# One region in place of five tanh buffers, in the additive attention of a two-layer block

## Chip, cores and metric

The kernel runs on one core of a Trainium2 chip. The metric is the device time of one execution in microseconds (us); less is better. Engines are named as in the profile: PE is TensorE (PEld its weight loads), DVE is VectorE, ACT is ScalarE, POOL is GpSimd, SP is SyncE, which issues most of the DMAs. All data is float32.

## The reference

`x` has shape (8, 64, 16, 128): 8 batches of N = 1024 tokens with 128 channels. Two layers follow each other, batch by batch except for the last step.

```python
# layer 0: attention with 8 heads over (m, g), two softmaxes, then a feed-forward part
scores = einsum('bhlfc,bhmgc->bhlfmg', q, k) / sqrt(c)
a = softmax(softmax(scores, axis=4), axis=5)
z = einsum('bhlfmg,bhmgc->bhlfc', a, v)          # then @ wo.T, + x, layer norm
x = layer_norm(relu(z1 @ w1.T + b1) @ w2.T + b2 + z1)

# layer 1: additive attention, for all pairs of tokens i, j
Wi = einsum('bnd,ed->bne', B, W)                 # B = layer norm of the tokens t
scores = einsum('d,bijd->bij', v, tanh(Wi[:, None] + Wi[:, :, None]))
t = t + softmax(scores, axis=-1) @ B

# then a recurrence over the tokens, y = sigmoid(wx_t + y @ V.T), with batch statistics
```

The costly part of layer 1 is the tanh of every pair of tokens. Since tanh(Wi_i + Wi_j) is the same for (i, j) and (j, i), the kernel computes only about half of the square.

## The kernel before

**Who orders the work.** Nothing is issued in a loop's order. `layer0`, `check_bounds`, `layer1` and `fetch_wx` only describe operations: `add` in `class Plan` takes for each the engines that may do it with a cost in us on each, a function that issues its instructions, what it reads and writes, and a priority. `Plan.emit` then plays the whole program through once, as the kernel is built. It keeps a modelled time for every engine, always takes the engine that can begin earliest and, of the operations that could begin on it within 0.15 us, the one with the least priority number, and issues it. What comes out is one fixed order of instructions for each engine; on the chip each engine works it off in order and waits where data or buffers aren't ready. Layer 0 of batch b+1 is thus woven into layer 1 of batch b.

**Buffers in the plan.** An operation with `take=` needs a buffer, one with `give=` frees it. A `Bank` names the buffers that it may choose from. `start_at` puts off an operation until the first of them is free in the plan, and `emit` takes the one that has been free longest:

```python
t = max(t, min(bank_free.get(c[0], 0.0) for c in take.of(e)))
...
take.name, take.tile = min(take.of(e), key=lambda c: bank_free.get(c[0], 0.0))
bank_free[take.name] = never
```

When the operation with `give=` is planned, the buffer counts as free from that operation's planned end, plus 0.6 us where PE does it. On the chip the real accesses to the columns decide: who writes columns waits for the matmuls that read them last.

**The pairs of tokens.** Tokens are in blocks of 128, `it` = 0 to 7. For block `it` only columns from its start on are needed, w = 1024 - 128 it of them. Four rows of a block (c = 0 to 3) are worked on at once, and k = max(1, 1024 // w) steps of r0 together; that is a *group*, `group` (L1006): 4k rows, whose first columns are left out as r0 grows (`begin`), so that a group has k(4w - 16 r0 - 6) columns for r0 over 0, and 4kw for r0 = 0. There are 172 groups in a batch, 1376 in all. A group goes through four steps:

1. It takes a tanh buffer `th` of 4N = 4096 columns (`slot`).
2. It is filled. Either POOL or DVE adds to `wiT` one column of it for each row (`add_rows`, L1039, for all k rows of one c; `add_row`, L1033, one row on DVE), or ACT does each row, sum and tanh in one instruction (`tanh_row`, L1029, the column as a bias). If ACT does row 0 it does all four; otherwise POOL and DVE share them.
3. If POOL or DVE filled it, ACT takes the tanh of the whole group in one instruction (`wide_tanh`, L1087).
4. PE multiplies each row by v (`times_v`, L1107), with results in the PSUM tile `sa`, and gives the buffer back.

**Stages.** In batches 1 to 6 the blocks are worked on in stages (0), (1, 7), (2, 6), (3, 5), (4), two blocks of a pair being interleaved. A stage ends with the Exp of its scores (`exps`, L1203, ACT). In batches 0 and 7 the stages are (4), (5, 7), (6), (0), (1), (2), (3), and the first three of batch 0 may use only three of the five buffers, since the other two hold the values of layer 0's eight heads then (`ths[3 + h // 4]` in `layer0`). The five buffers also hold four weights at the start (`early`) and x of all batches for `check_bounds`.

**Layer 0 beside it.** For each head and 128 tokens: scores on PE (L869), Exp on ACT (L872), sums and division on DVE (L876, L877, L880), a second Exp on ACT (L890), sums and reciprocal on DVE (L893, L894), a division on POOL (L904), transposes on PE (L783) with copies on DVE (L795), and the product with the values on PE (L918).

Of the kernel before, what the change touches and what calls it, by code (L numbers as in the profile page):

```python
# [15 lines left out]
P = 128  # L16
# [382 lines left out]
class Bank:  # L399
# [3 lines left out]
    def __init__(self, *choice, own=None):  # L403
        self.choice = choice
        self.own = own or {}
# [4 lines left out]
    def __call__(self):  # L410
        return self.tile


class Plan:

# [44 lines left out]
    def emit(self, slack=0.15, switch=0.1, stay=0.015):  # L460
        ops, by = self.ops, self.by
        after = [[] for _ in ops]
        left = []
        for n, o in enumerate(ops):
            before = o[4] | set(o[7])
            left.append(len(before))
            for d in before:
                after[d].append(n)
        engines = list(self.LATENCY)
        open_ = {e: [] for e in engines}  # L470
        free = dict.fromkeys(engines, 0.0)
        done = [0.0] * len(ops)
        began = [0.0] * len(ops)
        places = [None] * len(ops)
        mode = "full"
        bank_free = {}
        port_free = 0.0
        never = float("inf")
        self.order = []

        def ready_at(n, e):
            t = max((began[d] for d in ops[n][7]), default=0.0)
            for d in ops[n][4]:
                t = max(t, done[d] + (self.AGAIN if by[d] == e else self.LATENCY).get(by[d], 0.0))
            return t

        def start_at(n, t, e):
            take = ops[n][5]
            if take:
                t = max(t, min(bank_free.get(c[0], 0.0) for c in take.of(e)))  # L490
            if e == "POOL" or (e == "DVE" and ops[n][8]):
                t = max(t, port_free)
            return max(t, free[e])

        def release(n):
            where = ops[n][0]
            where = where() if callable(where) else where
            if where is None:
                began[n] = done[n] = ready_at(n, None)
                finish(n)  # L500
                return
            places[n] = {p[0]: (*p[1:], 0.0) for p in (where if isinstance(where, list) else [where])}
            for e in places[n]:
                open_[e].append((n, ready_at(n, e)))

        def finish(n):
            for a in after[n]:
                left[a] -= 1
                if left[a] == 0:
                    release(a)  # L510

        for n in [n for n, c in enumerate(left) if c == 0]:
            release(n)
        while any(open_.values()):
            first, e = min(
                (min(start_at(n, t, e) for n, t in open_[e]), i) for i, e in enumerate(engines) if open_[e]
            )
            assert first < never
            e = engines[e]
            n, start = min(  # L520
                ((n, s) for n, s in ((n, start_at(n, t, e)) for n, t in open_[e]) if s <= first + slack),
                key=lambda c: (ops[c[0]][2][0] + places[c[0]][e][1] + (stay if e == "PE" and ops[c[0]][3] != mode else 0), c[0]),
            )
            _, fn, _, m, _, take, give, _, port = ops[n]
            if take:
                take.name, take.tile = min(take.of(e), key=lambda c: bank_free.get(c[0], 0.0))
                bank_free[take.name] = never
            cost = places[n][e][0]
            if e == "PE":
                if m != mode:  # L530
                    cost += switch
                mode = m
            free[e] = start + (cost if e != "SP" else 0.2)
            if e == "POOL" or (e == "DVE" and port):
                port_free = start + cost
            began[n], done[n], by[n] = start, start + cost, e
            for q in places[n]:
                open_[q] = [c for c in open_[q] if c[0] != n]
            if give:
                bank_free[give.name] = done[n] + self.LATENCY[e]  # L540
            self.order.append((n, e, start, done[n]))
            fn(e)
            finish(n)
# [22 lines left out]
def fast_path(ctx: ExitStack, tc: tile.TileContext, a: dict, fits):  # L566
# [6 lines left out]
    NB, N, C = a["x"].shape  # L573
# [15 lines left out]
    work = main.enter_context(tc.tile_pool(name="work", bufs=1))  # L589
    psum = main.enter_context(tc.tile_pool(name="psum", bufs=1, space=PSUM))  # L590

    def tile_of(pool, name, shape):
        return pool.tile(shape, F32, tag=name, name=name)

    def ring(name, n, shape, pool=work):
        return [tile_of(pool, f"{name}{i}", shape) for i in range(n)]
# [17 lines left out]
        return t  # L614

    xTs = ring("xT", 2, [P, N])
    ths = ring("th", 5, [P, 4 * N])
    us = [wx[:, i, :] for i in range(2)]
    vps = [wx[:, 2 + i, :].rearrange("p (t c) -> p t c", c=C) for i in range(2)]
    aTs = ring("aT", 2, [P, NT, 2 * P])  # L620
# [16 lines left out]


    def early(k, name, eng):
        t = ths[k // 4][:, (k % 4) * N : (k % 4 + 1) * N].rearrange("p (h c) -> p h c", c=C)  # L640
        eng.dma_start(out=t, in_=a[name])
        return t

# [158 lines left out]
    def layer0(b):  # L802
# [16 lines left out]
        for n_part, part in enumerate(parts):  # L819
# [3 lines left out]
            for h in range(H):  # L823
                L0 = pace(n_part, h)

                u, vp, kvp = us[h % 2], vps[h % 2], ("vp", h % 2)
                if alone:
                    vp, kvp = ths[3 + h // 4][:, h % 4 * N : (h % 4 + 1) * N].rearrange("p (t c) -> p t c", c=C), ("vp0", h)
                for s in range(2) if part is None else (part,):
                    cols = slice(s * 512, (s + 1) * 512)  # L830

# [22 lines left out]
                for qt in qts:  # L854
                    L0 = pace(n_part, h + (qt - qts[0]) / len(qts))
                    i = (n_part * H + h) * len(qts) + qt - qts[0]
# [3 lines left out]
                    e, ke = e2[:, q, :], ("e", pair, q)  # L860
# [38 lines left out]
                    for q in range(2):  # L899
                        e, ke = e2[:, q, :], ("e", pair, q)  # L900
# [35 lines left out]
            for qh in range(2) if part is None else (part,):  # L936
# [4 lines left out]
                def raw(bank=bank):  # L941
# [4 lines left out]
                    take=bank, wait=[kg])  # L946
# [54 lines left out]
                add(("POOL", 2.2), affine2, r=[kg], w=[kg], pri=L0)  # L1001

    unused = stats[5][:, 3, 8:9]
    slots = [(f"th{s}", ths[s]) for s in range(5)]

    def group(it, at0, r0, k, wiT, all_wi, L1, ROWS, fillers, chain, left, both, first_half):  # L1006

# [5 lines left out]
        w = N - i0  # L1013
        g = count.setdefault("group", 0)
        count["group"] = g + 1
        slot = Bank(*slots[: 3 if first_half else 5])

        begin = [0 if r0 == 0 else 4 * r0 + c for c in range(4)]
        at = [k * sum(w - q for q in begin[:c]) for c in range(5)]

        def rows(c):
            return slot()[:, at[c] : at[c + 1]].rearrange("p (r n) -> p r n", r=k)
# [5 lines left out]
        def tanh_row(c, r):  # L1028
            nc.scalar.activation(rows(c)[:, r, :], wiT[:, i0 + begin[c] :], AF.Tanh, bias=w_i(c, r))  # L1029

        def add_row(c, r):

            nc.vector.tensor_scalar(  # L1033
                rows(c)[:, r, :], wiT[:, i0 + begin[c] :], w_i(c, r), 0.0, ALU.add, ALU.add, accum_out=unused
            )

        def add_rows(eng, c):
            shape = [P, k, w - begin[c]]
            eng.tensor_tensor(  # L1039
                rows(c), wiT[:, i0 + begin[c] :].unsqueeze(1).to_broadcast(shape),  # L1040
                w_i(c).unsqueeze(2).to_broadcast(shape), ALU.add,
            )
# [3 lines left out]
        work = {  # L1046
            "ACT": lambda c: (k * (0.18 + 0.833e-3 * (w - begin[c])), lambda: [tanh_row(c, r) for r in rows_of]),
            "POOL": lambda c: (0.27 + 1.62e-3 * k * (w - begin[c]), lambda: add_rows(nc.gpsimd, c)),
            "DVE": lambda c: (k * (0.21 + 1.05e-3 * (w - begin[c])), lambda: [add_row(c, r) for r in rows_of])
            if k < 4  # L1050
            else (0.15 + 1.04e-3 * k * (w - begin[c]), lambda: add_rows(nc.vector, c)),
        }
# [43 lines left out]
        for s0 in range(0, N, 512):  # L1096
            for c in range(4):
                s, s1 = max(s0, at0 + begin[c]), min(s0 + 512, at0 + w)
# [16 lines left out]
        n = -(-w // 512)  # L1115
# [18 lines left out]
    E_first, at = {}, 0  # L1134
# [153 lines left out]
    def check_bounds():  # L1288
# [1 line left out]

        cols, n2 = ET[:, 1, : 4 + 2 * H], ET[:, 2, : NB * NT]
        for b in range(NB):
            xb = ths[b // 4][:, b % 4 * N : (b % 4 + 1) * N].rearrange("p (t c) -> p t c", c=C)
            add(
                ("SP", 8.0),
                lambda _, b=b, xb=xb: nc.sync.dma_start(out=xb, in_=a["x"][b].rearrange("(t p) c -> p t c", p=P)),
                w=[("xn", b)], pri=LATE,
            )
            for t in range(NT):

                def square(_, xt=xb[:, t, :], j=b * NT + t):
                    nc.scalar.activation(xt, xt, AF.Square, accum_out=n2[:, j : j + 1])

                add(("ACT", 0.4), square, r=[("xn", b)], w=[("n2", b, t)], pri=LATE)
# [36 lines left out]
        for i, dst in enumerate((most, tot)):  # L1341
            through_bank(
                lambda bank, i=i: nc.tensor.matmul(
                    bank[0:1, :K], red[:, i : i + 1], ident[:K, :K], start=True, stop=True
                ), 0.3, ["red"],
# [17 lines left out]

    layer0(0)
    check_bounds()
    for b in range(NB):
        if b + 1 < NB:
# [38 lines left out]
    with tc.tile_pool(name="ps_w", bufs=2, space=PSUM) as ps_w, tc.tile_pool(  # L1406
# [22 lines left out]
        n = 0  # L1429
        for b in range(NB):  # L1430
            for g in range(2):
                pt = ps_t.tile([P, 4, C], F32, tag="yt", name="yt")
                for i in range(4):
                    t = 4 * g + i
# [75 lines left out]
```

## Time and profile before

| | us |
|---|---|
| median of 3 runs | 5395.53 (5393.81 to 5401.85) |
| the profiled execution | 5395.36, of which its span is 5393.6 |
| ACT busy | 5099.2 |
| PE busy | 5044.0 |
| DVE busy | 4933.6 |
| POOL busy | 4496.0 |
| wide tanh L1087, 953 instructions | 2629.0 |
| rows on ACT L1029, 2084 instructions | 1502.5 |
| rows on POOL L1039, 2268 instructions | 3318.7 |
| rows on DVE L1033, 1754 instructions | 1542.3 |

The profile is of one execution. The span runs from its first to its last instruction. The page gives the busy time of each engine, the same in 40 equal slices (135 us each), the chain of work that ended last, and the costliest groups of instructions with the idle time of the engine just before them and what ended it. The list of waits gives who waited for whom, in total, how often, and the longest. PE's ends are modelled, and busy PE isn't PE at its peak.

### The profile page before, as it was taken

To read this page: it belongs to the slowest core of one execution; us is meant where nothing else is said; L and a number is where in the kernel's file an instruction comes from. 1 tells how busy PE (TensorE), PEld (TensorE's weight loads), DVE (VectorE), ACT (ScalarE), POOL (GpSimd) and SP (SyncE) were. 2 spreads that over 40 slices of the span, in tenths; PEclk is the share of its full clock that TensorE was granted. 3 is DMA by queue.
4 is the path that set the end of the run, shared out by engine and by line. 5 is a ranking of instruction groups with operands and counts; after the bars stand their busy time and mean duration, and the time that the engine had idled before them with its cause. 6 is when DMAs were issued, how large, how long until landed. Compare 5 with 4: busy or idle time off the path is not lost.

```text
span 5393.6 us, 99434 instructions
## 1 busy us (share of the span) xinstructions
PE 5044.0 (94%) x39173; PEld 2771.6 (51%) x39173; DVE 4933.6 (91%) x8326; ACT 5099.2 (95%) x4190; POOL 4496.0 (83%) x3078
## 2 busy tenths in 40 slices
PE   8999999999999999999999999999999999995566
PEld 6655554555555455555555555545555455542125
DVE  7998989899999999899998999999998999999886
ACT  5489999999999999999999999999999999999994
POOL 2364779798989899899998989898898998996992
PEclk9999999999999999999999999999999999998999
DMA  2000000000000000000000000000000000000001
GB/s 62 1 5 1 1 1 5 1 9 1 1 5 6 4 1 1 5 9 1 1 5 5 5 1 1 5 5 5 1 1 3 7 1 1 1 30 8 1 1 68
DMA packets 27341, 37.73 MB, mean 7 GB/s; under 512 B 2512, under 2 KB 19280, under 8 KB 26864
## 3 DMA queue, kind: packets, MB, share of 16 engines
q1 hardware_dynamic: 24832, 27.99, 1.6%
q8 instruction: 310, 5.08, 0.4%
q10 hardware_dynamic: 1872, 3.16, 0.2%
q14 instruction: 167, 1.37, 0.1%
q0 software_dynamic: 160, 0.13, 0.0%
HBM read 19.22 MB, written 12.06 MB: 6 GB/s over the span
## 4 chain that ended last, share of the span: by engine, by line
PE 56%; ACT 19%; DVE 18%; issue 6%; POOL 1%; DMA 0%; DVEq 0%; ACTq 0%; SPq 0%; POOLq 0%
PE sa L1107 20%; PE m L918 11%; PE sc L869 10%; ACT th L1087 10%; PE m L783 6%; ACT th L1029 5%; DVE th L1033 5%; DVE stat_e L876 2%; DVE stat_e L893 2%; DVE wx L880 2%; ACT sc L872 2%; ACT wx L890 2%; PE m L1236 2%; DVE aT L795 2%; PE m L847 1%
## 5 line engine op out<-in xcount | busy, mean ns | idle before, releaser
L1039 POOL TENSOR_TENSOR th<-wiT 128x1024 f32<-128x1024 f32 (+54 forms) x2268 | 3318.7, 1500 | 318.2 <-PE sa L1107 298.8
L1087 ACT ACTIVATE th<-th 128x4096 f32<-128x4096 f32 (+55 forms) x953 | 2629.0, 2788 | 22.6 <-DVE th L1039 9.5
L1107 PE MATMUL sa<-th,vpat 128*32 128x512 f32 (+33 forms) x24576 | 2037.4, 462 | 235.6 <-ACT th L1087 223.3
L1033 DVE TENSOR_SCALAR_CACHE_REDUCE th<-wiT 128x512 f32<-128x512 f32 (+57 forms) x1754 | 1542.3, 879 | 156.7 <-PE sa L1107 40.3
L1029 ACT ACTIVATE th<-wiT 128x384 f32<-128x384 f32 (+60 forms) x2084 | 1502.5, 792 | 29.2 <-PE sa L1107 28.9
L1107 PEld LDWEIGHTS sa<-th,vpat 128*32 128x32 f32 x24576 | 662.8, 110 | 1372.1 <-issue 844.3
L904 POOL TENSOR_TENSOR wx<-wx,stat_e 128x1024 f32<-128x1024 f32 x512 | 983.9, 1944 | 389.4 <-DVE stat_e L894 320.8
L869 PE MATMUL sc<-xT,wx 128*128 128x512 f32 x2048 | 981.2, 604 | 11.3 <-DVE wx L880 10.7
L918 PE MATMUL m<-aT,wx 128*128 128x256 f32 x3584 | 823.7, 383 | 4.7 <-DVE aT L795 4.5
L918 PEld LDWEIGHTS m<-aT,wx 128*128 128x128 f32 x3584 | 668.1, 190 | 187.5 <-issue 48.0
L880 DVE TENSOR_TENSOR wx<-sc,stat_e 128x1024 f32<-128x1024 f32 x512 | 624.2, 1219 | 25.0
L876 DVE TENSOR_REDUCE stat_e<-sc 128x16 f32<-128x1024 f32 x512 | 619.7, 1210 | 25.8 <-ACT sc L872 25.3
L795 DVE COPY aT<-m 128x512 f32<-128x512 f32 x927 | 600.3, 674 | 36.7 <-PE m L783 34.3
L783 PEld LDWEIGHTS m<-ident,wx 128*128 128x128 f32 x3940 | 443.5, 141 | 326.0 <-issue 156.9
L893 DVE TENSOR_REDUCE stat_e<-wx 128x128 f32<-128x2048 f32 x256 | 583.2, 2278 | 19.1 <-ACT wx L890 18.4
L783 PE MATMUL m<-ident,wx 128*128 128x128 f32 x3940 | 562.6, 278 | 29.7 <-DVE aT L795 14.3
L872 ACT ACTIVATE sc<-sc 128x1024 f32<-128x1024 f32 x512 | 512.7, 1007 | 62.3 <-PE sc L869 56.0
L869 PEld LDWEIGHTS sc<-xT,wx 128*128 128x128 f32 x2048 | 354.7, 190 | 374.4 <-issue 329.3
L890 ACT ACTIVATE wx<-wx 128x2048 f32<-128x2048 f32 x256 | 487.7, 1905 | 30.1 <-DVE wx L880 29.9
L894 DVE RECIPROCAL stat_e<-stat_e 128x128 f32<-128x128 f32 x256 | 243.9, 953 | 8.8
L847 PEld LDWEIGHTS m<-Wvo,xT 128*128 128x128 f32 x1080 | 134.4, 192 | 53.0 <-issue 26.9
L847 PE MATMUL m<-Wvo,xT 128*128 128x128 f32 x1080 | 145.5, 281 | 4.4 <-DVE aT L795 2.4
(183 smaller groups left out, 2887.0 us busy)
## 6 DMA issues: line engine op xcount, KB each, us to landing
xT<-in_xt_dram SPq DMA_DIRECT2D x8, 512.0 KB, 3.6
th<-in_x_dram SPq DMA_DIRECT2D x8, 512.0 KB, 6.8
parked<-X SPq DMA_DIRECT2D x16, 256.0 KB, 2.3
xr<-parked SPq DMA_DIRECT2D x8, 512.0 KB, 8.1
parked_wx<-bT SPq DMA_DIRECT2D x14, 256.0 KB, 2.0
wx<-parked_wx SPq DMA_DIRECT2D x7, 512.0 KB, 4.3
out_dram<-ot ACTq DMA_DIRECT2D x8, 256.0 KB, 2.1
out_dram<-ot SPq DMA_DIRECT2D x8, 256.0 KB, 2.8
```

The costliest lines, as they stand in the source:

```text
L783: nc.tensor.transpose(bank[:, i * P : (i + 1) * P], s, ident)
L795: nc.vector.tensor_copy(dst, src)
L869: nc.tensor.matmul(sc[:, cols], u[:, qt * P : (qt + 1) * P], xT[:, cols], start=True, stop=True)
L876: nc.vector.tensor_reduce(r1, sc.rearrange("p (m g) -> p g m", g=G), AX.X, ALU.add)
L880: nc.vector.tensor_tensor(e3, sc3, r1.unsqueeze(1).to_broadcast([P, M, G]), ALU.mult)
L904: nc.gpsimd.tensor_tensor(e3, e3, r2[:, q, :].unsqueeze(2).to_broadcast([P, M, G]), ALU.mult)
L918: nc.tensor.matmul(bank()[:, :256], vp[:, t, :], aT[:, t, :], start=t == 0, stop=t == NT - 1)
L1029: nc.scalar.activation(rows(c)[:, r, :], wiT[:, i0 + begin[c] :], AF.Tanh, bias=w_i(c, r))
L1033: nc.vector.tensor_scalar(rows(c)[:, r, :], wiT[:, i0 + begin[c] :], w_i(c, r), 0.0, ALU.add, ALU.add, accum_out=unused)
L1039: eng.tensor_tensor(rows(c), wiT[:, i0 + begin[c] :].unsqueeze(1).to_broadcast(shape), w_i(c).unsqueeze(2).to_broadcast(shape), ALU.add,)
L1087: nc.scalar.activation(slot()[:, a:z], slot()[:, a:z], AF.Tanh)
L1107: nc.tensor.matmul(sa[32 * c : 32 * c + 32, s:s1], vpat[:, 31 - r0 - r : 63 - r0 - r], rows(c)[:, r, s - at0 - begin[c] : s1 - at0 - begin ...
```

## The change

The five tiles `ths` become one tile `th` of the same 20N columns. A `Room` keeps a list of spans of it, each with the time from which it is free in the plan. A group takes a `Span` with just as many columns as it has: `place` looks, from every border between spans, for neighbouring spans that together are long enough, and returns the place with the earliest start and, among equals, the lowest column. `hold` cuts the spans to fit, `free` sets the time from which the taken one is free again. `Bank` gets methods of the same names, so that `emit` asks either kind; what it does for PSUM banks stays the same. The limit of three buffers in the first stages becomes a limit of 12N columns.

```diff
+class Room:
+    def __init__(self, tile, size):
+        self.tile = tile
+        self.spans = [[0, size, 0.0]]
+
+    def place(self, n, now, top):
+        best = None
+        for i, (a, _, _) in enumerate(self.spans):
+            t, z = now, a
+            for _, z, free in self.spans[i:]:
+                t = max(t, free)
+                if z - a >= n:
+                    break
+            if z - a >= n and a + n <= top and (best is None or (t, a) < best):
+                best = (t, a)
+        return best
+
+    def hold(self, a, n):
+        spans = []
+        for x, z, t in self.spans:
+            if x < a:
+                spans.append([x, min(z, a), t])
+            if z > a + n:
+                spans.append([max(x, a + n), z, t])
+        spans.append([a, a + n, float("inf")])
+        self.spans = sorted(spans)
+
+    def free(self, a, t):
+        for span in self.spans:
+            if span[0] == a:
+                span[2] = t
+
+class Span:
...
+    def __call__(self):
+        return self.room.tile[:, self.at : self.at + self.n]
+
+    def when(self, e, t, bank_free):
+        return self.room.place(self.n, t, self.top)[0]
+
+    def hold(self, e, t, bank_free):
+        self.at = self.room.place(self.n, t, self.top)[1]
+        self.room.hold(self.at, self.n)
...
@@ Plan.emit
-                t = max(t, min(bank_free.get(c[0], 0.0) for c in take.of(e)))
+                t = take.when(e, t, bank_free)
...
-                take.name, take.tile = min(take.of(e), key=lambda c: bank_free.get(c[0], 0.0))
-                bank_free[take.name] = never
+                take.hold(e, start, bank_free)
...
-                bank_free[give.name] = done[n] + self.LATENCY[e]
+                give.free(done[n] + self.LATENCY[e], bank_free)
@@ fast_path
-    ths = ring("th", 5, [P, 4 * N])
+    room = 20 * N
+    th = tile_of(work, "th", [P, room])
+    ring_room = Room(th, room)
...
-        t = ths[k // 4][:, (k % 4) * N : (k % 4 + 1) * N].rearrange("p (h c) -> p h c", c=C)
+        t = th[:, k * N : (k + 1) * N].rearrange("p (h c) -> p h c", c=C)
...
-                    vp, kvp = ths[3 + h // 4][:, h % 4 * N : (h % 4 + 1) * N].rearrange("p (t c) -> p t c", c=C), ("vp0", h)
+                    vp, kvp = th[:, (12 + h) * N : (13 + h) * N].rearrange("p (t c) -> p t c", c=C), ("vp0", h)
...
-    slots = [(f"th{s}", ths[s]) for s in range(5)]
@@ group
-        slot = Bank(*slots[: 3 if first_half else 5])
...
         at = [k * sum(w - q for q in begin[:c]) for c in range(5)]
+        slot = Span(ring_room, at[4], 12 * N if first_half else 20 * N)
@@ check_bounds
-            xb = ths[b // 4][:, b % 4 * N : (b % 4 + 1) * N].rearrange("p (t c) -> p t c", c=C)
+            xb = th[:, b * N : (b + 1) * N].rearrange("p (t c) -> p t c", c=C)
```

More of the change, by code (lines that the diff above doesn't have):

```diff
@@ L411, in __call__, with free, __init__, when @@
         return self.tile
+    def when(self, e, t, bank_free):
+        return max(t, min(bank_free.get(c[0], 0.0) for c in self.of(e)))
+    def hold(self, e, t, bank_free):
+        self.name, self.tile = min(self.of(e), key=lambda c: bank_free.get(c[0], 0.0))
+        bank_free[self.name] = float("inf")
+    def free(self, t, bank_free):
+        bank_free[self.name] = t
+class Room:
[27 more added lines that the diff above has]
+class Span:
+    def __init__(self, room, n, top):
+        self.room = room
+        self.n = n
+        self.top = top
+    def __call__(self):
+        return self.room.tile[:, self.at : self.at + self.n]
+    def when(self, e, t, bank_free):
+        return self.room.place(self.n, t, self.top)[0]
+    def hold(self, e, t, bank_free):
+        self.at = self.room.place(self.n, t, self.top)[1]
+        self.room.hold(self.at, self.n)
+    def free(self, t, bank_free):
+        self.room.free(self.at, t)
 class Plan:
```

## The prediction

> **What bounds the kernel now.** I read the page first: which engine is full, and for how much of the span.
>
> ```profile
> PE 5044.0 (94%) x39173; PEld 2771.6 (51%) x39173; DVE 4933.6 (91%) x8326; ACT 5099.2 (95%) x4190; POOL 4496.0 (83%) x3078
> ...
> PE   8999999999999999999999999999999999995566
> ...
> ACT  5489999999999999999999999999999999999994
> ```
>
> Four engines are nearly full, and ACT is fullest. The slices show that its idle time lies in the first 400 us and the last 100. I then took busy times by stage, cutting the span at the Exp that ends each stage (L1203). Over batches 1 to 6, which are 3730 us, ACT is idle for 31 us, PE for 93, DVE for 221 and POOL for 329. So ACT is the bound there: time falls only if ACT waits less or has less to do. After 4860 us no layer 0 is left, PE drops to 5 or 6 tenths and waits for ACT's tanh, so ACT is the bound there too.
>
> Next, ACT's own groups, and who fills the tanh buffers:
>
> ```profile
> L1039 POOL TENSOR_TENSOR th<-wiT 128x1024 f32<-128x1024 f32 (+54 forms) x2268 | 3318.7, 1500 | 318.2 <-PE sa L1107 298.8
> L1087 ACT ACTIVATE th<-th 128x4096 f32<-128x4096 f32 (+55 forms) x953 | 2629.0, 2788 | 22.6 <-DVE th L1039 9.5
> ...
> L1033 DVE TENSOR_SCALAR_CACHE_REDUCE th<-wiT 128x512 f32<-128x512 f32 (+57 forms) x1754 | 1542.3, 879 | 156.7 <-PE sa L1107 40.3
> L1029 ACT ACTIVATE th<-wiT 128x384 f32<-128x384 f32 (+60 forms) x2084 | 1502.5, 792 | 29.2 <-PE sa L1107 28.9
> ```
>
> A group is filled in one of two ways. POOL or DVE adds its rows and ACT takes one wide tanh (L1087), or ACT does every row itself with a bias (L1029). The last column is the one that matters here: all three fillers wait for "PE sa L1107", the matmuls that read a buffer and thereby free it. The list of waits gives their counts:
>
> ```profile
> POOL th L1039 <- PE sa L1107: 298.8, 143, 11.3
> ...
> DVE th L1033 <- PE sa L1107: 40.3, 62, 2.4
> ...
> ACT th L1029 <- PE sa L1107: 28.9, 25, 4.3
> ```
>
> The second number is how many waits, the third the longest. POOL loses most, 298.8 us in 143 waits, but it isn't the bound. ACT loses only 28.9 us in 25 waits, of some 521 groups that it fills (2084 rows by four). So the buffers are short, and the shortage costs mostly where it is cheap.
>
> **What the Trainium skill says.** "Perfetto Trace Analysis", section Optimization Strategy, says a gap that repeats on the engine that should be saturated can mean too little buffer space. Here the repeating gap is on POOL (298.8 us), hardly on the saturated ACT (28.9). Its section Optimizing Scalar/DVE Operations gives ScalarE a fixed cost of about 93 ns per instruction on SBUF, with larger operations better when the engine is saturated. The trace agrees for the wide tanh: fitting the start-to-start distance of ACT instructions to their columns gives 0.833 ns per column plus 97 ns for L1087. The row form L1029 has the same slope but 187 ns. Its section Identifying Dependency Chains says that an instruction which waits on several engines may get EventSemaphore instructions ahead of it; the trace has 341 of 17 ns ahead of L1029, on ACT's queue.
>
> **The change, part by part.** It removes no arithmetic and adds none: 4.22 million columns of tanh remain, as do all matmuls. The early weights, the eight x tiles of the bounds check and batch 0's values keep their columns, because slot s was columns 4sN to 4(s+1)N; their DMAs (x: 6.8 us to landing) don't move. The first stages keep 12N, that is the old three slots. All that costs nothing, and no cover is needed. What changes is how many groups are held at once, and the order that the planner writes from it.
>
> How many fit: a group has k(4w - 16 r0 - 6) columns, its first r0 apart. The means by tile are 3842 (it 0), 3330, 2818, 2306, 3605 (it 4), 2581, 3179 and 2524. The region has 20480. So it=0 and it=4 still get five (5.3 and 5.7). The pairs (1,7), (2,6) and (3,5) get about 6.3, 7.1 and 8.5, weighted by their counts, less holes, since a place must be contiguous. A stage of (3,5) takes 138 us for 48 groups, 2.9 us each, so five buffers let a group live 14 us and eight 23. A (3,5) group by POOL takes 4.7 us for four rows (fitted like ACT's: 0.2 us and 1.67 ns a column, 577 columns), 2.1 for the wide tanh and, on average of all 1376 groups, 1.5 for its matmuls (2037 us of L1107), 8.3 us besides queueing at three nearly full engines: five is tight, seven less so.
>
> The gain, as a ceiling. (a) ACT's own waits outside it=0 and it=4: 28.9 less 4.1 in those stages is 25 us, straight off the bound. (b) POOL's waits outside them: 298.8 less 86 (29 + 10 in batches 1 to 6, 20 + 14 in batch 0, 7 + 5 in batch 7) is 212 us. At 1.5 us a row instruction that is 142 more, 35 groups that ACT needn't fill. What ACT saves on a group: four rows cost 4 x 187 = 748 ns of fixed time, one wide tanh 97, so 0.65 us; 35 groups are 23 us. (c) DVE likewise: 29 us at 0.96 us a row (879 ns and its 82 ns accumulator read) is 30 rows, 7 groups, 5 us. Sum 53 us. ACT's saving is cashed only while another engine has room: PE has 93 us idle in batches 1 to 6, so it covers this, with little left.
>
> I take half, 27 us, from this: the old planner took the buffer that had been free longest, while the new search takes the earliest possible start and, among equals, the lowest column. Columns that PE released last moment in the plan are thus reused although older free ones exist, and every delay of PE against the plan becomes a wait again. Half is a choice; nothing measured fixes it.
>
> Unseen costs. A group now overlaps columns of two or three old ones, so its rows may need waits of their own: at most 2084 - 341 = 1743 more of 17 ns, 30 us, if each reached the ACT engine; at the other end fewer than now, a gain up to 341 x 17 ns = 6 us. The page puts ACT's queue at 0% of the chain, so I take 0 and keep 30 for the range. When it=0 begins (4096 columns, five of them fill the region exactly) among the leftovers of smaller groups, only four may fit for one round: seven times some 20 us with a lookahead of four; bounded by a few us each, between 0 and 20 us in all, taken as part of the half. In the tail (after 4860 us) ACT is already at full wide tanhs; 0 there.
>
> What is queued behind a wait: ACT works in order, so a row that waits holds up the score exponentials (L872, L890) and the wide tanhs behind it, for which PE waits. A POOL row that waits holds up the divide L904, and the transposes on PE behind that. With (b) gone, what is late next is POOL's other wait, for DVE's reciprocal (L904, 321 us, over half of it before 405 us).
>
> **Sum.** The profiled execution took 5395.4 us (span 5393.6 and 1.8 around it), which is the median of the runs (5395.5). Less 27: **5369 us**.
>
> **Rivals.**
> 1. The ceiling: all 53 us come, 5342. For it: the waits are many and short, as a buffer shortage would give. Against: the lowest-column rule, and holes.
> 2. No difference: PE at 97.5% in batches 1 to 6 becomes the bound as soon as ACT gets lighter, or holes eat the room and the region holds five again, so that the change doesn't do what it says. 5395. Against: PE's busy time is modelled and includes matmuls that stand beside each other.
> 3. Slower: the lowest-column rule lands on ACT. Now 25 of ACT's 521 groups wait, 1.16 us each (28.9 / 25). If the ones that ACT fills get just-freed columns more often, each wait stops the bound itself. It decides from 27 / 1.16 = 23 more waits, 48 groups in 521. At 65 waits, one group in eight, it costs 40 x 1.16 = 46 us against 14 that the other fillers still bring (half of b and c): 5395 + 32 = 5427. For it: PE is so full that it must often run behind the plan, and the old rule protected against just that. Against: POOL, idle for 329 us, is usually first at freed columns, and ACT is rarely idle when they come free.
>
> **How the numbers follow.** About 0.2%, 11 us, is what can be told from no change. The main case has 0.45, the ceiling 0.15, no difference 0.13, slower 0.27. So faster is 0.60, within 0.2% 0.13, slower 0.27. The range: below 5332 (ceiling and 10 us) 0.06 is left, above 5428 (rival 3 at 65 waits) 0.12. The likeliest case alone spans 5350 to 5384.
>
> **What would show it.** Right: POOL's wait for PE sa at the filling line falls from 299 us to about 190, ACT's from 29 to some 15; L1029 has about 85 rows fewer and the POOL and DVE lines as many more; ACT's busy time falls by about 14 us; the saving lies in stages (1,7), (2,6) and (3,5) and not in it=0. Wrong: L1029 rows increase, ACT's wait for PE sa rises over 55 us, or ACT is idle in the middle while PE is full.

## The result, and the profile after

The changed kernel takes 5387.4 us (median of 20 runs), the one before 5395.2 in the same comparison: ratio 0.9983, 95% interval 0.9976 to 0.9990. That is 8 us or 0.17% less, where 27 were forecast. The direction was right, the size was not. By the prediction's own yardstick, that 0.2% is the least that can be told, it is no difference; the interval over 20 runs of each does leave out 1.

The page of the changed kernel, busy times and the groups that answer to those shown of before (the columns are again count, busy us, mean ns, idle time before it and what ended most of it):

```profile
span 5388.9 us, 99191 instructions
...
PE 5048.0 (94%) x39173; PEld 2782.9 (52%) x39173; DVE 4961.5 (92%) x8448; ACT 5093.6 (95%) x4180; POOL 4536.0 (84%) x3114
...
L1107 POOL TENSOR_TENSOR th<-wiT 128x536 f32<-128x536 f32 (+58 forms) x2304 | 3342.3, 1486 | 244.6 <-PE sa L1175 222.8
L1155 ACT ACTIVATE th<-th 128x2740 f32<-128x2740 f32 (+54 forms) x971 | 2661.2, 2771 | 23.2 <-DVE th L1107 12.3
...
L1101 DVE TENSOR_SCALAR_CACHE_REDUCE th<-wiT 128x512 f32<-128x512 f32 (+60 forms) x1822 | 1587.4, 871 | 140.1 <-PE sa L1175 21.9
L1097 ACT ACTIVATE th<-wiT 128x440 f32<-128x440 f32 (+58 forms) x2056 | 1462.7, 782 | 15.1 <-PE sa L1175 14.9
```

L1107, L1155, L1101 and L1097 are the old L1039, L1087, L1033 and L1029. The waits for columns fell as they should: POOL's for PE sa from 299 to 223 us, DVE's from 40 to 22, ACT's from 29 to 15. But ACT does only 28 rows fewer (2056 for 2084), and its busy time falls by 5.6 us, which is about all that the span lost. ACT's idle time is as long as before: 5388.9 less 5093.6 is 295 us, and it was 294. So the 14 us that ACT no longer waits for columns came back as other waits. From the list of ACT's waits, of after:

```profile
ACT sc L942 <- PE sc L939: 71.0, 60, 5.6
...
ACT wx L960 <- DVE wx L950: 21.3, 18, 4.2
...
ACT th L1097 <- PE sa L1175: 14.9, 9, 5.9
...
ACT E L1271 <- PE sa L1175: 10.5, 9, 2.1
```

The first Exp of layer 0 (L942, the old L872) waits 71 us for its matmuls, 15 more than the 56 before, and the Exp that ends a stage (L1271) 9 more than its 1.4. The second Exp (L960) waits 9 less than its 29.9. POOL's case is alike:

```profile
POOL wx L974 <- DVE stat_e L964: 360.4, 118, 40.6
POOL th L1107 <- PE sa L1175: 222.8, 134, 9.9
POOL E L1277 <- ACT E L1271: 60.6, 15, 16.1
```

Of the 76 us that POOL waits less for columns it waits 40 more for DVE's reciprocal (was 321) and 27 more for ACT's Exp (was 34), and it does only 36 more row instructions.

Where this lies shows in the table of windows, the span cut at the Exps that end batch 0, batch 6 and batch 7, before and then after. The columns are the stretch, its length, busy us with instructions for PE, PEld, DVE, ACT and POOL, and then the granted TensorE clock (1.00 is full speed), the DMA share and GB/s:

```profile
0.00:1078.80 1078.80, 1023.61 (x6628) 617.34 (x6629) 963.46 (x1410) 904.48 (x1091) 690.33 (x462) 1.00 0.03 10
1078.80:4809.40 3730.60, 3637.42 (x28718) 1979.36 (x28716) 3487.62 (x5845) 3695.94 (x2772) 3397.49 (x2327) 1.00 0.01 4
4809.40:5296.70 487.30, 311.02 (x3282) 109.47 (x3282) 425.63 (x909) 470.43 (x234) 404.74 (x285) 0.94 0.01 3
```

```profile
0.00:1065.50 1065.50, 1022.21 (x6622) 617.75 (x6623) 961.25 (x1420) 899.93 (x1072) 718.05 (x482) 0.99 0.03 10
1065.50:4802.20 3736.70, 3634.58 (x28723) 1986.18 (x28721) 3518.95 (x5949) 3687.21 (x2744) 3411.73 (x2347) 0.99 0.01 4
4802.20:5293.10 490.90, 319.11 (x3282) 113.05 (x3282) 424.36 (x917) 478.05 (x269) 402.73 (x281) 0.92 0.01 3
```

Batch 0 is 13 us shorter. Batches 1 to 6, where most of the gain was forecast, are 6 us longer: ACT has 9 us less to do there (3687 for 3696) and is idle 15 us longer (49.5 for 34.7). Batch 7 is 4 us longer. The granted clock is lower in all three stretches.

The chain of work that ended last, by engine, before and then after:

```profile
PE 56%; ACT 19%; DVE 18%; issue 6%; POOL 1%; DMA 0%; DVEq 0%; ACTq 0%; SPq 0%; POOLq 0%
```

```profile
PE 67%; DVE 15%; ACT 12%; issue 4%; POOL 1%; DMA 0%; DVEq 0%; SPq 0%; ACTq 0%; POOLq 0%
```

More than half of it is PE's already before, and after it is two thirds.

The instructions of each group can be followed through the trace by their order, from the first row to the last matmul. Before, 3.9 groups are held on average, and five at once for 31% of the time. After, it is 4.1, and more than five for 10% of the time. The room is there, and it is used seldom.

### The profile page after: what moved, and what is told of

Read it like the earlier page. It is cut to its first block, busy times and chain, and to the rows that moved or that the text cites. A ratio compares the mean times of both kernels' runs of the same rounds, so it can differ in the third digit from the quotient of the medians.

```text
span 5388.9 us, 99191 instructions
## 1 busy us (share of the span) xinstructions
PE 5048.0 (94%) x39173; PEld 2782.9 (52%) x39173; DVE 4961.5 (92%) x8448; ACT 5093.6 (95%) x4180; POOL 4536.0 (84%) x3114
## 4 chain that ended last, share of the span: by engine, by line
PE 67%; DVE 15%; ACT 12%; issue 4%; POOL 1%; DMA 0%; DVEq 0%; SPq 0%; ACTq 0%; POOLq 0%
PE sa L1175 24%; PE m L988 13%; PE sc L939 13%; PE m L853 8%; ACT th L1155 6%; DVE th L1101 6%; ACT th L1097 3%; DVE stat_e L963 2%; PE m L917 2%; PE m L1304 2%; DVE stat_e L946 2%; DVE wx L950 1%; PE m L903 1%; DVE aT L865 1%; PE m L1035 1%
## 5 line engine op out<-in xcount | busy, mean ns | idle before, releaser
L1107 POOL TENSOR_TENSOR th<-wiT 128x536 f32<-128x536 f32 (+58 forms) x2304 | 3342.3, 1486 | 244.6 <-PE sa L1175 222.8
L1155 ACT ACTIVATE th<-th 128x2740 f32<-128x2740 f32 (+54 forms) x971 | 2661.2, 2771 | 23.2 <-DVE th L1107 12.3
L1175 PE MATMUL sa<-th,vpat 128*32 128x512 f32 (+32 forms) x24576 | 2030.6, 462 | 212.5 <-ACT th L1155 187.2
L1101 DVE TENSOR_SCALAR_CACHE_REDUCE th<-wiT 128x512 f32<-128x512 f32 (+60 forms) x1822 | 1587.4, 871 | 140.1 <-PE sa L1175 21.9
L1097 ACT ACTIVATE th<-wiT 128x440 f32<-128x440 f32 (+58 forms) x2056 | 1462.7, 782 | 15.1 <-PE sa L1175 14.9
L942 ACT ACTIVATE sc<-sc 128x1024 f32<-128x1024 f32 x512 | 513.7, 1008 | 75.9 <-PE sc L939 71.0
L960 ACT ACTIVATE wx<-wx 128x2048 f32<-128x2048 f32 x256 | 487.2, 1903 | 21.6 <-DVE wx L950 21.3
```

The lines of the kernel that those rows point to most:

```text
L1101: nc.vector.tensor_scalar(rows(c)[:, r, :], wiT[:, i0 + begin[c] :], w_i(c, r), 0.0, ALU.add, ALU.add, accum_out=unused)
L1107: eng.tensor_tensor(rows(c), wiT[:, i0 + begin[c] :].unsqueeze(1).to_broadcast(shape), w_i(c).unsqueeze(2).to_broadcast(shape), ALU.add,)
L1155: nc.scalar.activation(slot()[:, a:z], slot()[:, a:z], AF.Tanh)
L1175: nc.tensor.matmul(sa[32 * c : 32 * c + 32, s:s1], vpat[:, 31 - r0 - r : 63 - r0 - r], rows(c)[:, r, s - at0 - begin[c] : s1 - at0 - begin ...
```

## The experiments

Theories at the start. **S**: the region is seldom used beyond five groups, so there was little to win. **R**: the lowest-column rule makes fillers wait for PE and eats the gain. **P**: ACT wins at the columns and loses at PE's scores. **O**: any change makes the planner write another order, and an order has luck of its own. Ratios are to the kernel before in the same comparison, with 95% intervals; its median was 5398 to 5401 us there.

**low5**: before, with the lowest free buffer instead of the one free longest; the order of instructions stays.

```diff
-                take.name, take.tile = min(take.of(e), key=lambda c: bank_free.get(c[0], 0.0))
+                tanh = take.choice[0][0] == "th0"
+                take.name, take.tile = min(
+                    take.of(e),
+                    key=lambda c: (max(bank_free.get(c[0], 0.0), start), c[0]) if tanh else (bank_free.get(c[0], 0.0), 0),
+                )
```

> The kernel before with its five buffers and its order of instructions on every engine; only which of the buffers that are free in the plan a group takes is changed, from the one free longest to the lowest. Theory R (the lowest-column rule makes fillers wait for PE and eats the gain): slower than before by 10 us or more, ACT's wait for PE sa at the rows rises from 29 us to over 50, POOL's from 299 to over 350. Theory S (the region is seldom used beyond five groups, so there was little to win) and theory P (what ACT gained at the buffers it lost waiting for PE's scores): no difference beyond 6 us, since the choice matters only when more than one buffer is free.

Measured 5398.7 us, ratio 1.0005 (0.9997 to 1.0013). POOL's wait rose to 330 us, ACT's to 31, in a profiled execution that took 10 us more than the median. So the rule does cost POOL, some 31 us of waiting, and the kernel nothing that can be told: R had asked for 10 us or more, and for over 50 us of waiting on ACT.

**oldest**: the region, among equal starts the place that has been free longest.

```diff
-                t = max(t, free)
+                t, old = max(t, free), max(old, free)
...
-            if z - a >= n and a + n <= top and (best is None or (t, a) < best):
-                best = (t, a)
+            if z - a >= n and a + n <= top and (best is None or (t, old, a) < best):
+                best = (t, old, a)
```

> The kernel after with one edit: among places with the same earliest start it takes the one whose columns have been free longest instead of the lowest. Theory R: the missing 19 us come, about 5370, and POOL's and ACT's waits for PE sa fall by a third or more. Theories S and P: 5387 within 8 us. Theory O (any other order of the planner moves the time by some 10 us either way, and the 8 us may be luck of one order) allows 5375 to 5400 without a pattern in the waits.

5390.0 us, 0.9990 (0.9981 to 0.9998). POOL's wait fell to 170 us and ACT's to 11.5, about a quarter less than in after, where R had asked for a third; and the time did not follow. The planner's order changed here too.

**room18**: the later groups may use 18N.

```diff
-slot = Span(ring_room, at[4], 12 * N if first_half else 20 * N)
+slot = Span(ring_room, at[4], 12 * N if first_half else 18 * N)
```

> The kernel after, the groups of the later stages limited to 18N of the 20N columns. Theory S: what room is worth shows in this slope; if two N matter little because five groups are seldom exceeded, it is under 12 us slower than after; if buffers are a real limit where five groups of 4096 must fit (it=0 and it=4, which then hold four), it is 20 to 40 us slower, and POOL's wait for PE sa rises above before's 299 us. Theory P: under 8 us slower, since PE bounds anyway. Theory O: anything within 10 us.

5412.5 us, 1.0025 (1.0014 to 1.0037): 23 us slower than after. POOL's wait was 296 us, just under before's 299, with 2104 rows on ACT. That room counts isn't shown by it, since the limit also makes the planner write another order, and the runs below put orders of the region up to 38 us apart. S, that there is little to win, is neither supported nor refuted by it.

**after_slack13**: after, another order by one number of the planner.

```diff
-    def emit(self, slack=0.15, switch=0.1, stay=0.015):
+    def emit(self, slack=0.13, switch=0.1, stay=0.015):
```

> The kernel after, with the planner's slack of 0.15 us set to 0.13: no instruction is added or removed, the same rules, another order. Theory O: the time moves by 5 us or more from 5387, either way. If orders don't matter (R, S, P alone): within 4 us of after.

5349.0 us, 0.9912 (0.9898 to 0.9925): 38 us faster than after, by an edit with no bearing on buffers. Its page has the two lines of the middle again:

```profile
PE 5020.8 (94%) x39173; PEld 2772.2 (52%) x39173; DVE 4940.8 (92%) x8449; ACT 5080.7 (95%) x4115; POOL 4483.3 (84%) x3096
...
L1097 ACT ACTIVATE th<-wiT 128x744 f32<-128x744 f32 (+51 forms) x2000 | 1477.9, 809 | 5.9 <-PE sa L1175 5.4
```

ACT does 84 rows fewer than before, is busy 18.5 us less, and waits 5 us for columns. These are marks that the prediction named (85 rows, 14 us); but POOL's wait is still 246 us, far from the 190 that it named. The first Exp waits 50 us for PE and not 71. O is alive, so the pairs had to be made: the same number in both kernels.

**before_slack13** and **before_slack14** (the edit above in the kernel before, 0.13 and 0.14), **after_slack14**, and **after_stay02** and **before_stay02** (`stay=0.02`, slack 0.15):

> The kernel before with the planner's slack set to 0.13 as in after_slack13, five equal buffers. If the 38 us that after gained by it come from a better slack, this one gains as much, about 5357. Theory O (each order has its own luck, and a change of the slack is only another throw): somewhere between 5375 and 5415, with no relation to after's gain. Theory S then says that the region's own worth is the mean of several such pairs, some 15 to 25 us.

> The kernel before, slack 0.14: another order by the same rules. Theory O: 5380 to 5410, another value than before and before_slack13 by 5 us or more. If order is no cause of spread with equal buffers: within 4 us of before.

> The kernel after, slack 0.14. Theory O: between 5345 and 5395, not after's 5387 but nearer the middle of these. If after's order at 0.15 was typical of the region and after_slack13 a lucky one, 5380 to 5390; if after's was the unlucky one, 5345 to 5375.

> The kernel after, slack 0.15 as it was, but the planner's charge for changing PE's mode set from 0.015 to 0.02: a change that has nothing to do with the tanh buffers. Theory O: another time by 5 us or more, either way, 5350 to 5400. If orders hardly matter: within 4 us of 5387.

> The kernel before with the charge for changing PE's mode at 0.02, the fourth pair with after_stay02. Theory O: 5385 to 5410. With the other three it gives the mean of five equal buffers over four orders, expected at 5395 to 5402, against 5373 of the region over the same four.

| order | five buffers | region | region against five buffers |
|---|---|---|---|
| slack 0.15 | 1 | 0.9983 (0.9976 to 0.9990) | -0.17% |
| slack 0.13 | 5405.4 us, 1.0010 (1.0003 to 1.0017) | 5349.0 us, 0.9912 (0.9898 to 0.9925) | -0.98% |
| slack 0.14 | 5391.5 us, 0.9987 (0.9980 to 0.9994) | 5366.5 us, 0.9936 (0.9922 to 0.9949) | -0.51% |
| stay 0.02 | 5398.8 us, 0.9998 (0.9992 to 1.0005) | 5387.3 us, 0.9978 (0.9969 to 0.9988) | -0.20% |

The region is faster in all four, by 0.47% or 25 us on average, from 9 to 53; four values that far apart fix the mean to some 10 us either way (its standard error). The order of after gains least, with `stay=0.02` close to it. That last edit moved neither kernel by more than 1 us, where O had expected 5 or more; the slack moved both. Over their profiles, the region has 61 rows fewer on ACT (2026 for 2087), ACT is busy 12 us less (5087 for 5099) and idle 14 us less (284.5 for 298.8), and waits for columns 11 us instead of 26.

Where the time goes, in the profiles of the four pairs, cut as above (us, region less five buffers), and the granted clock, the mean of all runs of a kernel in these experiments:

| order | batch 0 | batches 1 to 6 | batch 7 and the end | clock, five buffers | clock, region |
|---|---|---|---|---|---|
| slack 0.15 | -13 | +6 | +2 | 0.9885 | 0.9854 |
| slack 0.13 | -12 | -36 | -7 | 0.9851 | 0.9896 |
| slack 0.14 | -22 | +4 | -9 | 0.9867 | 0.9874 |
| stay 0.02 | -12 | +8 | -15 | 0.9873 | 0.9872 |
| mean | -15 | -5 | -7 | 0.9869 | 0.9874 |

Batch 0 is shorter in all four, batches 1 to 6 in one. ACT's idle time in batches 1 to 6 doesn't fall on average, 41.1 us for 41.0. POOL's waits for columns in these batches do what was forecast in the stages of two blocks, 60 us for 137 on average, and the reverse in stages (0) and (4), where five large groups fill the region: 86 for 46.

The clock is a rival explanation that no run here isolates. Among runs of one kernel, with one order, a lower clock goes with a longer time in all but two of the kernels here: of after's 20 runs, 13 at 0.985 have a mean of 5388.9 us and 7 at 0.986 one of 5383.9; of the runs of before, 9 at 0.987 have 5402.5 and 10 at 0.990 have 5396.4. That is 2 to 5 us for 0.001. Which causes which isn't shown. By that estimate the clock of after, 0.003 under that of before, is worth 6 to 15 us, a good part of the 19 that are missing, and the high clock of after_slack13 part of its lead. On average over the four pairs the clock is the same, so it isn't what the 25 us come from.

**alternate** and **alternate_again** (the same kernel twice): before, its planned order unchanged; in each buffer the groups lie at the low and the high end by turns (`n` is the group's number of columns).

```diff
     def __call__(self):
+        if self.n:
+            a = 4096 - self.n if self.high else 0
+            return self.tile[:, a : a + self.n]
         return self.tile
...
                 bank_free[take.name] = never
+                if take.n:
+                    take.high = not self.high.get(take.name, True)
+                    self.high[take.name] = take.high
```

> The kernel before, its order of instructions unchanged on every engine, five buffers of 4096 columns; but in each buffer the groups lie at the low and the high end by turns, so that a group smaller than a buffer overlaps only part of the columns of the one before it, and its first or last rows needn't wait for the matmuls on the rest. Theory W (waits for columns on the chip are themselves what costs): ACT's wait for PE sa at the rows falls from 29 us to about 15, POOL's from 299 to about 220, and the time by 10 us or more, to 5388 or less. Theory Q (the gain comes only through the order that the planner writes when it has more room: fewer rows on ACT, other turns): the waits fall too, but the time stays within 5 us of before's.

> The kernel of the run alternate once more (before's order, groups at the low and high end of each buffer by turns), since its six times lay between 5373 and 5390 and its profile, of the 5387 one, showed ACT's wait for PE sa unchanged at 29.5 us. Theory W (waits for columns on the chip cost by themselves): again 15 to 25 us under before, and a profile with POOL's wait about 35 us lower. If the 20 us were chance: within 8 us of before.

5378.9 us, 0.9956 (0.9943 to 0.9968), and 5380.4 us, 0.9964 (0.9950 to 0.9977). So 20 us or so come with no operation moved in the planned order. The second's page, after the first line of before's:

```profile
span 5393.6 us, 99434 instructions
```

```profile
span 5378.6 us, 98600 instructions
...
PE 5039.8 (94%) x39173; PEld 2774.1 (52%) x39173; DVE 4932.6 (92%) x8326; ACT 5096.5 (95%) x4190; POOL 4492.2 (84%) x3078
...
L1048 POOL TENSOR_TENSOR th<-wiT 128x1024 f32<-128x1024 f32 (+54 forms) x2268 | 3313.9, 1495 | 272.1 <-PE sa L1116 259.9
L1042 DVE TENSOR_SCALAR_CACHE_REDUCE th<-wiT 128x512 f32<-128x512 f32 (+57 forms) x1754 | 1542.7, 880 | 127.7 <-PE sa L1116 37.7
L1038 ACT ACTIVATE th<-wiT 128x384 f32<-128x384 f32 (+60 forms) x2084 | 1500.7, 790 | 28.2 <-PE sa L1116 27.9
```

The counts of operations are those of before to the last one. POOL waits 39 us less, ACT at its own rows only 1 us less. W had asked for half there, so it holds for the time and not for the way. ACT's idle time is 282 us for 294, in small parts: 5 us less at the second Exp for DVE's division, 5 less at the wide tanh for DVE's rows.

But the edit changes one thing more. The whole program has 834 instructions fewer, all of them semaphore instructions, which stand in an engine's queue ahead of an operation. On DVE's queue ahead of its rows, before and then alternate_again:

```profile
L1033 DVEq EVENT_SEMAPHORE  x994: 21/21/3045, 303.8 to 5292.6; - x199
```

```profile
L1042 DVEq EVENT_SEMAPHORE  x687: 21/21/2412, 303.6 to 5274.9; - x172
```

DVE's idle time before its rows falls from 157 to 128 us, and only 3 of these 29 are waits for PE. In the trace of before, a row that follows another row begins a median of 122 ns after the other's end (with its accumulator read) where a semaphore instruction stands ahead (787 rows), and 36 ns after it where none does (316 rows). In alternate_again 541 rows have one in this place, 246 fewer, and at the difference of 86 ns that is some 21 us of DVE's time (an estimate from these gaps). So two things came together, POOL's earlier columns and DVE's lighter queue, and the runs don't part them. low5 speaks for the second: there POOL's wait moved by 31 us the other way, DVE's idle time before its rows stayed at 158 us, and the time didn't change either.

**alternate_slack13** and **alternate_slack14**: the same edit in before_slack13 and before_slack14.

> before_slack13 (5405 us) with the groups at the low and high end of each buffer by turns, its order unchanged. Theory W: 10 to 25 us under it, 5380 to 5395, whatever the order is. Theory Q (the region gains through the order alone): within 5 us of 5405.

> before_slack14 (5391.5 us) with the groups at the low and high end of each buffer by turns, its order unchanged. Theory W: 10 to 25 us under it, 5367 to 5382. Theory Q: within 5 us of 5391.5. Together with the run before, it says how much of the region's mean of 25 us over four orders can come from earlier columns alone.

5381.8 us, 0.9969 (0.9958 to 0.9981), against 1.0010 without the edit: 22 us. 5377.2 us, 0.9961 (0.9948 to 0.9975), against 0.9987: 14 us. The gain is there in three orders, with 19 us on average, and DVE has 307, 306 and 293 semaphore instructions fewer ahead of its rows. Moving the groups helps with no change of the planned order, against Q; that it helps by earlier columns, as W says, isn't shown, nor that the region gains in this way.

**oldest_slack13** and **oldest_slack14**: the longest-free rule in two of the other orders.

> The region with the place whose columns have been free longest, slack 0.13; its partner with the lowest column is after_slack13 (5349 us). Theory R (the lowest-column rule costs by itself): 10 us or more under 5349. Theory O (another rule is first of all another order): anywhere from 5345 to 5385, without regard to the partner; after_slack13 being the best of its four, rather above it.

> The same with slack 0.14; its partner with the lowest column is after_slack14 (5366.5 us). Theory R: 10 us or more under 5366. Theory O: anywhere from 5350 to 5395, without regard to the partner; the mean over the three pairs (slack 0.15, 0.13, 0.14) then doesn't differ from the lowest column's 5368 by more than its spread.

5372.1 us, 0.9952 (0.9938 to 0.9965), and 5413.2 us, 1.0029 (1.0018 to 1.0040). Over three parameters the longest-free rule has 0.9990, 0.9952 and 1.0029, the lowest column 0.9983, 0.9912 and 0.9936. R gets no support: the rule that was suspected isn't the slower one in these. The second lies above all that O had allowed (5350 to 5395). In oldest_slack14 ACT has fewer rows (2032) than in before, and is idle for 327 us; there it waits 27 us for DVE's fills (L1155 for L1107, seven waits of up to 9.6 us) where before waits 9.5. It also has the lowest granted clock of all kernels here, 0.984 on average.

**after_best**, **before_best** and **oldest_best**: of sixty orders each (slack and stay drawn at random), the one that the planner expects to end first: after with 0.118 and 0.005, before with 0.11 and 0.021, the longest-free rule with 0.086 and 0.018.

> The kernel after with slack 0.118 and stay 0.005, an order chosen from sixty because the planner itself expects it to end earliest. If what makes an order good is what the planner can see, it is as good as after_slack13 or better, 5335 to 5355. If luck on the chip is another matter, it lies anywhere from 5350 to 5390.

> The kernel before with slack 0.11 and stay 0.021, chosen from sixty in the same way with five equal buffers. If the region is worth some 25 us beyond the luck of an order, this stays 15 us or more above after_best and above after_slack13, at 5365 to 5385. If a good order is all there is to it, the two kernels are within 8 us of each other.

> The region with the place whose columns have been free longest, slack 0.086 and stay 0.018, chosen from sixty orders as the one that the planner expects to end earliest. If a good order by the planner's own reckoning is what counts: 5340 to 5365, like after_slack13 and after_best, and the rule for the place makes no difference to that. If the lowest-column rule costs by itself: under 5345.

before_best 5390.9 us, 0.9977 (0.9968 to 0.9986); after_best 5359.7 us, 0.9919 (0.9907 to 0.9932); oldest_best 5336.6 us, 0.9882 (0.9867 to 0.9898). Against the mean of their four orders, the pick has 0.2% with five buffers and 0.3% with the region; against the mean of its three, the longest-free rule has 1.1%. These are single picks, and after_best is no faster than after_slack13, which wasn't picked. before_best was expected at 5365 to 5385 and is above it. oldest_best is under 5345, which its expectation had called a sign for R; at equal parameters, above, the sign isn't confirmed. It is the fastest kernel of all, 64 us under before and some 50 under the change. Its page has ACT busy for 5081.1 us of 5335.6, idle for 254.5, and 2004 rows on ACT.

## Why the prediction was wrong in size

**What bounds.** ACT was taken as the one bound, off which saved time comes straight. The runs don't bear that out. The chain that ended last is 56% PE's before and 67% after, against 19 and 12% for ACT, and in one and the same order the time goes with the clock of TensorE. (The windows above give ACT 34.7 us of idle time in batches 1 to 6 before and DVE 243, not 31 and 221; nothing turns on that.) Both count, then, though PE's ends are modelled. That is rival 2, which had 0.13, and under 0.2% is what it forecast. Its waits were there too: in this order ACT waits 15 us longer for PE's scores. That isn't the general rule: over the four orders of the region ACT waits 71, 50, 57 and 61 us for them, over the four with five buffers 56, 64, 49 and 57.

**Step (a), ACT's own waits straight off the bound: failed.** They fell by 14 us, which is the half of 25 that was taken, and to the 15 that was named as the sign. But ACT's idle time went from 294 to 295 us: the gain went into other waits, most of them for PE. Over four orders idle time does fall by 14 us, but none of that is in batches 1 to 6.

**Steps (b) and (c), POOL's and DVE's waits turned into rows taken from ACT: too large.** Forecast 85 rows and 14 us of ACT's busy time, measured 28 rows and 5.6 us; over four orders it is 61 rows and 12 us. The way differs as well. POOL waits 76 us less for columns, where half of 212 was counted on, and does 36 more row instructions, where half of 142 was. DVE does 68 rows more; at 0.96 us each these are 65 us, far more than its 18 us of shorter waits for columns. Counted in groups (1376 less the wide tanhs), ACT fills 405 for 423; the prediction's 521 took four rows for every group, though groups with k over 1 have more.

**The term that was missing.** The sum was made as if the order of before stayed and only waits shrank. The prediction said that the change alters the order that the planner writes, and gave that no number. It is as large as the effect: with equal rules and an idle change of one constant, five buffers lie between 5391 and 5405 us and the region between 5349 and 5387. Each order also has a clock of its own. The mean gain over four orders, 25 us, is near the 27 of the sum, but in part by luck: the mean is known to some 10 us only, half of the ceiling was a choice, and the time isn't gained where the sum had it. So the failed step is the forecast of one order by waits alone, without the spread of orders and with every wait of ACT as pure loss. The likeliest case, 5350 to 5384, should have been wider by some 20 us.

**Where the gain lies.** Forecast in stages (1,7), (2,6) and (3,5). The waits fell there, as said, and the time didn't: batches 1 to 6 got slower by 6 us and batch 0 faster by 13, and three of the four orders have these signs. POOL's longer waits in stages (0) and (4), 40 us on average, are a term that the prediction had left inside its half, at 0 to 20 us. The capacities of 6.3 to 8.5 groups were right as capacities, but room isn't use: only 10% of the time more than five groups are held.

**Rival 3** had its mechanism tested and not found. The lowest-column rule raises POOL's waits (low5) without a cost that can be told, and the longest-free rule isn't better over three orders.

**What stays open.** Why batch 0 gains isn't known, nor what the 19 us of the alternating ends come from, POOL's columns or DVE's semaphores. How much of the spread between orders is the clock and how much are the waits wasn't parted. The region with an order held fixed couldn't be tried, since the place of a group enters the plan.

## What to carry to other kernels

When a planner or compiler writes the order, a change to what it may assume is two changes: the mechanism, and a new throw of the order. Measure a few neutral variations of both kernels before a difference of half a per cent is credited or blamed, and compare the granted clocks of the runs as well. Picking the order is a step of its own, worth 0.2% and more here. Moving data within a buffer can change how many semaphore instructions an engine gets: count them before the gain is put down to shorter waits. Before costing more buffer space, count how many buffers are in use at once over the span, and how long all of them are.

## What the runs showed of the hardware

The granted TensorE clock belongs to the order as well as to the run. In the traces it is a row of short stretches, 3.4 us or a multiple, at half speed. In before and alternate_again, with the same planned order, many fall at the same places of the program: at 438, 1861, 3581 and 4482 us in the one, at 437, 1854, 3574 and 4475 us in the other. before has 24 such stretches, after 31. Among runs of one kernel, 0.001 of mean clock went with 2 to 5 us of time.

On DVE, a semaphore instruction between two rows went with a longer gap than the 21 ns of its own record: 122 ns from the end of one row to the start of the next, and 36 ns without one (medians in before). Where another kind of instruction stood ahead of the row, no such difference shows.

Bringing consecutive groups to opposite ends of the same buffers, with the same operations planned in the same order on every engine, was worth 14 to 22 us. It came with 39 us less waiting on POOL and with 834 semaphore instructions fewer; which of them counted isn't shown.
